# A planned hybrid transformer kernel: new charges and handoffs in the planner, and buffer fills moved from GpSimd to ScalarE

## The chip, the core and the metric

The kernel runs on one core of one Trainium2 chip. The metric is the device time of one launch in microseconds. Before the change the median of three runs is 515.56 us (514.37 to 515.59).

A core has a matrix engine (TensorE, PE in the profile, with its weight loads as PEld), a vector engine (VectorE, DVE), an activation engine (ScalarE, ACT), a general engine (GpSimd, POOL) and a queue that issues transfers (SyncE, SP). Each works through its own list of instructions in order, and waits at the head of its list for the semaphores of the others.

## What is computed

An input of 8 sequences x 256 tokens x 128 features, all in fp32, goes through eight residual layers. Cut to what matters:

```python
x = x + causal_attention(layernorm(x))      # one head of width 64, softmax
x = x + relu_ffn(layernorm(x))              # 128 -> 512 -> 128, with a layernorm at its end
x = x + linear_attention(layernorm(x))      # no softmax
x = x + relu_ffn(layernorm(x))
x = x + retention(layernorm(x))             # 16 heads, decay mask, gate
x = x + silu_ffn(layernorm(x))              # 128 -> 384 -> 128, weights from int32
x = x + softmax_attention(layernorm(x))     # 16 heads of width 8, LoRA weights
x = x + silu_ffn(layernorm(x))
```

## The kernel before, in words

**Tiles.** The 16 tiles of 128 tokens are held in four groups of four tiles, so that a group is two sequences. Each group has its buffer `x0` to `x3` (128 x 512) and goes through all eight layers as one thread, `layers(g)`. Within a layer a thread splits into more threads, such as one per sequence. PSUM is eight banks of 128 x 512; SBUF work buffers are handed out from named stores.

**The planner.** The order of the instructions is found in Python while the kernel is built. Every thread is a generator. `step(engine, us)` asks for a turn on an engine and says how long it will hold it; `either` names two engines and takes the one that is free first; `get` and `put` take buffers from a store and give them back. `Plan.run` keeps for each engine the time at which it is free, takes the earliest possible step, prefers ACT steps that need no table change and then the lower rank (group 0 first, the one-time work with rank LAST last), and lets the thread emit its instructions there. A step that follows one on another engine may start only after the first engine's entry in `HANDOFF`. What is emitted is a fixed list for each engine; the times of the plan are gone by then. So the charges do not make an instruction faster or slower: they decide which instruction stands before which on its engine, which of two engines an `either` takes, and, through the time at which a buffer comes free, which buffer and how many are taken.

**What matters for the change.**

- `constants()` (started at 8.0 us of the plan with rank LAST) fills the buffers of the later layers with ones and zeros on GpSimd: two triangles of `chunk_mul` (L379, L380), three `r_values` and three `l_values` of 128 x 576 (L388), and two halves each of two `r_spread` and two `l_spread`, 128 x 1024 a half (L392).
- `layernorm()`: statistics on DVE (L467, L468), four small GpSimd instructions for the reciprocal root (L470 to L473), and one instruction a tile on ACT (L479) or DVE (L484).
- `copied()` (L372) moves a PSUM bank to SBUF on ACT or DVE, whichever the plan has free first.
- `causal_attention()` is the first layer: weights L527 and L540, scores L562, mask L567, maxima L571, exponentials L574, transposes L581.
- `ffn_relu()` (L659, L672), `retention()` (its tiled products L795, L853, L875, L883) and `ffn_silu()` (L985, L991, L1001) follow.
- `pairs_of_scores()` is one thread for the 16-head attention of all groups. Scores of two heads are one item; an item needs two banks, and it exists twice: once for the maxima (`maxima`, L1092 on DVE) and once for the exponentials (`exponentials`, L1126 on ACT). A scoring step at L1071 takes two items, that use all four 32-row strips of PE, or one item, that uses two of them. While other groups are still at work a step with two items waits for four banks; in the last group (`todo["alone"]`) it takes two items only if more than one bank is free at that moment of the plan, and one item otherwise. A bank counts as free `LEEWAY` after its reader's step. `weighted()` (L1143) multiplies the exponentials with the values.

Each fp32 matmul stands in the profile as two records, so that a step with one item is 8 records at L1071 and a step with two items is 16.

Of the kernel before, what the change touches and what calls it, by code (L numbers as in the profile page):

```python
# [33 lines left out]
P = 128  # L34
# [28 lines left out]
HANDOFF = {PE: 0.3, ACT: 0.2, DVE: 0.2, POOL: 0.25, SP: 2.3}  # L63
TABLE_LOAD = 1.3
LEEWAY = 0.4
# [45 lines left out]
class Plan:  # L111
# [4 lines left out]
    def __init__(self):  # L116
        self.free = {e: 0.0 for e in (PE, ACT, DVE, POOL, SP)}
        self.steps = {e: [] for e in self.free}
        self.stores, self.untils, self.sleeping = [], [], []
        self.table = None  # L120
        self.current = None
        self.count = 0
        self.now = 0.0
# [25 lines left out]
    def resume(self, th, value):  # L149
# [12 lines left out]
        if kind == "step":  # L162
            for e, us, table in want[1]:
                self.steps[e].append((th.after(e), th, self.count, us, table))
        elif kind == "get":
# [18 lines left out]
    def run(self):  # L184
        self.go = []
        while True:
# [45 lines left out]
            if table not in (None, self.table):  # L232
                us += TABLE_LOAD
                self.table = table
            th.t, th.last = start + us, e
# [6 lines left out]
def step(engine, us, table=None):  # L242
    return ("step", ((engine, us, table),))


def either(*choices):
    return ("step", tuple((e, us, None) for e, us in choices))
# [19 lines left out]
def hybrid(ctx: ExitStack, tc: tile.TileContext, t: dict, out: bass.AP):  # L267
# [57 lines left out]
    nc.gpsimd.memset(minus_half, -0.5)  # L325

# [43 lines left out]
    def copied(dst, src, us):  # L370
        e = yield either((ACT, us), (DVE, us + 0.02))
# [3 lines left out]
    def constants():  # L375
# [8 lines left out]
        for store in (r_values, r_spread, l_values, l_spread):  # L384
            for _, _, tl in list(store.items):
                if tl.shape[1] == 2:
                    yield step(POOL, 0.6)
                    nc.gpsimd.memset(tl, 1.0)  # L388
                else:
                    for c in range(2):  # L390
                        yield step(POOL, 0.95)
                        nc.gpsimd.memset(tl[:, :, c, :], float(c))  # L392
        made["constants"] = True

    def causal_weights():
# [3 lines left out]
        yield step(PE, 0.5)  # L399
        nc.tensor.matmul(ps[:, :P], a_t[:, 0, :], a_t[:, 1, :], start=True, stop=True)  # L400
        nc.tensor.matmul(ps[:, P : 2 * P], a_t[:, 2, :], a_v2, start=True, stop=True)
        yield step(DVE, 0.6)
# [5 lines left out]
    def linear_weights():  # L408
# [3 lines left out]
        yield step(PE, 0.3)  # L412
        nc.tensor.matmul(ps[:, :P], b_tp[:, 1, :], b_tp[:, 0, :], start=True, stop=True)
        yield step(DVE, 0.3)
# [4 lines left out]
    def retention_weights():  # L419

        for w in (w_ret_vg, b_ret_v):
            yield step(DVE, 0.9)
# [8 lines left out]
    def silu_weights():  # L431
        ws = []
        for wi in (wi_gate, wi_up, wi_down):
            w = wi.bitcast(F32)
            yield step(DVE, 0.75)
# [5 lines left out]
    def softmax_weights():  # L441
# [3 lines left out]
        yield step(PE, 0.7)  # L445
# [4 lines left out]
        yield step(DVE, 0.8)  # L450
# [8 lines left out]
    def layernorm(src, y):  # L459
# [5 lines left out]
        for i in range(nt):  # L465
            yield step(DVE, 0.45)
            nc.vector.bn_stats(stats[:, i, :], src[:, i, :])  # L467
            nc.vector.bn_aggr(mv[:, i, :], stats[:, i, :])  # L468
        yield step(POOL, 1.05 + 0.18 * nt)
# [5 lines left out]
        def half(tiles):  # L475
            for i in tiles:
                e = yield either((ACT, 0.49), (DVE, 0.38))
# [14 lines left out]
    def transposed(y):  # L492
# [4 lines left out]
        yield step(PE, 0.02 + 0.11 * nt)  # L497
        for i in range(nt):
            nc.tensor.transpose(ps[:, i * P : (i + 1) * P], y[:, i, :], ident)  # L499
        yield from copied(yT[:, : nt * P], ps[:, : nt * P], 0.16 + 0.11 * nt)  # L500
# [14 lines left out]
    def add_row_to(g, row):  # L515
        yield step(POOL, 1.27)
        nc.gpsimd.tensor_tensor(x[g], x[g], tokens(row, NT), ALU.add)

    def add_to(g, tiles, ps):
        xs = flat(x[g][:, tiles, :])  # L520
        yield step(DVE, 0.09 + 0.135 * (tiles.stop - tiles.start))
# [10 lines left out]
    def causal_attention(g):  # L532
# [4 lines left out]
        def queries():  # L537
# [3 lines left out]
            yield from copied(q[:, :N], ps, 0.6)  # L541
            put(bank, ps)

        def value():
            ps = yield get(bank)
            yield step(PE, 0.86)
            by_tiles(ps, w[:, 1, :], yT)
            yield from copied(values[:, :N], ps, 0.6)
            put(bank, ps)

        def sequence(b):
# [14 lines left out]
            yield step(DVE, 0.48)  # L566
            nc.vector.tensor_tensor(p[:, : 3 * P], ps[:, : 3 * P], causal_add, ALU.add)  # L567
            put(bank, ps)
            yield step(DVE, 0.55)
            for i, (q0, lo, hi) in enumerate(blocks):  # L570
                nc.vector.tensor_reduce(nmax[:, i : i + 1], p[:, lo:hi], AX.X, ALU.max, negate=True)  # L571
            yield step(ACT, 1.3, "exp")
# [6 lines left out]
            yield step(PE, 0.34)  # L579
            for i in range(3):  # L580
                nc.tensor.transpose(ps[:, i * P : (i + 1) * P], p[:, i * P : (i + 1) * P], ident)  # L581
            yield from copied(pT[:, : 3 * P], ps[:, : 3 * P], 0.48)
            put(bank, ps)
            put(work, p)
            yield step(DVE, 0.17)
            nc.vector.reciprocal(sums, sums)
            ps = yield get(bank)
            yield step(PE, 0.65)
# [6 lines left out]
            yield step(DVE, 0.55)  # L595
# [15 lines left out]
    def linear_attention(g):  # L611
# [4 lines left out]
        for left in (None, b_g, made["linear"]):  # L616
            ps = yield get(bank)
            yield step(PE, 0.86 if left is None else 0.45)
# [12 lines left out]
            yield from copied(m[:, : 2 * D], ps[:, : 2 * D], 0.37)  # L631
            put(bank, ps)
        ps = yield get(bank)
        yield step(PE, 0.86)
# [9 lines left out]
    def ffn_relu(g):  # L644
# [5 lines left out]
        def biases():  # L650
            yield step(POOL, 1.27)
# [3 lines left out]
        def up(c):  # L655
# [4 lines left out]
            e = yield either((ACT, 0.69), (DVE, 0.67))  # L660
# [6 lines left out]
        def down(tiles):  # L667
            ps = yield get(bank)
            for n, i in enumerate(tiles):
                yield step(PE, 0.88)  # L670
# [5 lines left out]
            yield step(DVE, 0.35)  # L676
# [10 lines left out]
        yield step(POOL, 1.27)  # L687
        nc.gpsimd.tensor_tensor(y4, y4, tokens(gamma, NT), ALU.mult)
        yield step(DVE, 0.62)
# [3 lines left out]
    def spread_heads(qk, b, spread):  # L693

        for i in range(4):
            yield step(SP, 0.5)
# [17 lines left out]
    def retention(g):  # L714
# [4 lines left out]
        def rotated(i):  # L719
# [17 lines left out]
            e = yield either((POOL, 1.27), (DVE, 0.62))  # L737
# [3 lines left out]
        def gated(c):  # L741
# [5 lines left out]
            yield step(ACT, 0.62, "silu")  # L747
# [3 lines left out]
        def value(b):  # L751
            v = yield get(r_values)

            def part(m):
                ps = yield get(bank)
                yield step(PE, 0.45)
# [5 lines left out]
                yield step(DVE, 0.35)  # L762
# [10 lines left out]
        def scores(b, s):  # L773
# [4 lines left out]
            def masked(i, ps):  # L778
                yield step(DVE, 0.62)
# [7 lines left out]
            for i2 in range(2):  # L787
                ps = yield get(bank, 2)
                yield step(PE, 0.95)
# [14 lines left out]
        def states(b, v, state):  # L804
# [3 lines left out]
            yield step(PE, 0.24)  # L808
# [575 lines left out]
```

## Time and profile before

| | us |
|---|---|
| median of three runs | 515.56 |
| the profiled execution | 516.39 |
| its span, first to last instruction | 514.7 |
| PE busy | 465.5 (90%) |
| DVE busy | 354.2 (69%) |
| ACT busy | 238.9 (46%) |
| POOL busy | 144.4 (28%) |
| mean granted PE clock | 0.933 of full |

Busy time is the sum of an engine's instruction spans; the ends of matmuls are modelled. The granted clock is the share of its full clock that PE was given; at half of it a matmul takes about twice as long. A bracket such as `[0.17 <-POOL small L472]` at the end of a timeline line is the idle time of that engine just before the instruction, and what ended it.

### The profile page before, as it was taken

The numbers are of one execution on the slowest core, as the hardware profiler recorded it, in microseconds if no ns is written. First come the engines' busy times: TensorE is split into PE (matmuls) and PEld (weight loads), VectorE is DVE, ScalarE is ACT, GpSimd is POOL, SyncE is SP. The second block draws the span as 40 slices with busy tenths as digits, with TensorE's granted clock in tenths as the row PEclk, the third lists the DMA queues.
The fourth block names the chain that finished last, engine by engine and source line by source line (L and its number), as shares of the span: only waits on it lengthen the run. The fifth ranks groups of instructions, "written<-read, shape, count | busy, mean of one in ns | idle before, by whom it ended". The sixth has DMA issues, their size and how long they took to land.

```text
span 514.7 us, 13048 instructions
## 1 busy us (share of the span) xinstructions
PE 465.5 (90%) x5340; PEld 320.9 (62%) x5340; DVE 354.2 (69%) x985; ACT 238.9 (46%) x477; POOL 144.4 (28%) x259
## 2 busy tenths in 40 slices
PE   2779889999779998899999999999799979999996
PEld 1666767757647667547666656676476647765654
DVE  6979885889696669959648986745975643850233
ACT  3245447343335152338656285554338465135561
POOL 6805388576334161332120020320011030010011
PEclk9979989999989999969999999999979999655899
DMA  8100000003003002001000102011000003000000
GB/s 293 62 2 1 1 1 1 0 1 43 6 0 43 3 19 29 1 7 31 16 20 4 23 11 33 4 36 24 1 2 22 12 2 54 3 1 2 11 1 21
DMA packets 8043, 10.90 MB, mean 21 GB/s; under 512 B 1000, under 2 KB 6888, under 8 KB 7984
## 3 DMA queue, kind: packets, MB, share of 16 engines
q1 hardware_dynamic: 7904, 9.94, 8.6%
q8 instruction: 42, 0.69, 0.6%
q14 instruction: 17, 0.14, 0.1%
q10 hardware_dynamic: 80, 0.13, 0.1%
HBM read 4.56 MB, written 1.05 MB: 11 GB/s over the span
## 4 chain that ended last, share of the span: by engine, by line
PE 69%; DVE 22%; issue 3%; POOL 2%; ACT 1%; DMA 1%; SPq 0%; POOLq 0%; DVEq 0%; ACTq 0%
PE bank L1071 16%; PE bank L1143 6%; PE bank L659 5%; PE bank L985 5%; DVE small L1092 4%; PE bank L1001 4%; PE bank L991 4%; PE bank L672 3%; PE bank L795 3%; DVE work L484 3%; PE bank L853 3%; PE bank L499 2%; DVE small L467 2%; PE bank L527 2%; DVE small L468 2%
## 5 line engine op out<-in xcount | busy, mean ns | idle before, releaser
L1071 PE MATMUL bank<-l_spread 32*128 32x256 f32 x1024 | 104.3, 443 | 3.6 <-DVE small L1092 3.2
L1092 DVE TENSOR_REDUCE small<-bank 128x2 f32<-128x512 f32 x128 | 80.3, 682 | 27.8 <-PE bank L1071 27.6
L1126 ACT ACTIVATE probs<-bank 128x512 f32<-128x512 f32 x128 | 68.0, 599 | 48.3 <-PE bank L1071 44.7
L1071 PEld LDWEIGHTS bank<-l_spread 32*128 32x128 f32 x1024 | 66.7, 205 | 33.1 <-issue 12.9
L470 POOL TENSOR_SCALAR small<-small 128x4 f32<-128x4 f32 (+1 forms) x44 | 10.8, 246 | 265.4 <-DVE small L468 264.4
L372 ACT COPY work<-bank 128x512 f32<-128x512 f32 (+3 forms) x76 | 36.2, 481 | 85.6 <-PE bank L499 24.7
L479 ACT ACTIVATE work<-x,small 128x128 f32<-128x128 f32 x71 | 31.2, 488 | 29.1 <-POOL small L473 28.9
L472 POOL TENSOR_TENSOR small<-small,mhalf 128x4 f32<-128x4 f32 (+1 forms) x44 | 43.2, 982 | 0.0
L372 DVE COPY work<-bank 128x512 f32<-128x512 f32 (+3 forms) x36 | 19.8, 555 | 26.2 <-PE bank L1143 12.8
L467 DVE BATCH_NORM_STATS2 small<-x 128x6 f32<-128x128 f32 x128 | 34.6, 270 | 4.0 <-DMA x<-in_x 3.7
L499 PE MATMUL bank<-ident,work 128*128 128x128 f32 x128 | 25.1, 306 | 12.5 <-ACT work L479 9.3
L484 DVE TENSOR_SCALAR work<-x,small 128x128 f32<-128x128 f32 x57 | 30.4, 747 | 5.9 <-POOL small L472 5.9
L1143 PE MATMUL bank<-probs,l_values 128*32 128x256 f32 x512 | 33.6, 398 | 0.2 <-DVE work L780 0.2
L985 PE MATMUL bank<-work,c_ints 128*128 128x256 f32 (+1 forms) x72 | 30.0, 535 | 3.5 <-ACT work L372 1.6
L468 DVE BATCH_NORM_AGGREGATE small<-small 128x2 f32<-128x6 f32 x160 | 29.1, 182 | 5.6
L659 PE MATMUL bank<-work,c_relu 128*128 128x512 f32 x64 | 31.5, 617 | 0.9 <-ACT work L372 0.9
L672 PEld LDWEIGHTS bank<-c_relu,work 128*128 128x128 f32 x256 | 30.1, 192 | 2.6 <-issue 1.9
L672 PE MATMUL bank<-c_relu,work 128*128 128x128 f32 x256 | 31.4, 277 | 0.1
L993 DVE TENSOR_TENSOR work<-bank,work 128x256 f32<-128x256 f32 (+1 forms) x36 | 17.6, 507 | 18.4 <-PE bank L991 18.2
L499 PEld LDWEIGHTS bank<-ident,work 128*128 128x128 f32 x128 | 15.7, 149 | 23.2 <-ACT work L479 13.6
L1001 PEld LDWEIGHTS bank<-c_ints,work 128*128 128x128 f32 x192 | 23.9, 191 | 5.7 <-issue 3.2
L1001 PE MATMUL bank<-c_ints,work 128*128 128x128 f32 x192 | 26.7, 283 | 0.8 <-DVE work L993 0.8
(146 smaller groups left out, 807.1 us busy)
## 6 DMA issues: line engine op xcount, KB each, us to landing
r_spread<-wide SPq DMA_DIRECT2D x32, 64.0 KB
l_spread<-wide SPq DMA_DIRECT2D x32, 64.0 KB
out<-x SPq DMA_DIRECT2D x8, 128.0 KB
c_retention_qk<-in_retention_qk SPq DMA_DIRECT2D x1, 770.0 KB
x<-in_x SPq DMA_DIRECT2D x3, 256.0 KB
c_retention_vo<-in_retention_vo SPq DMA_DIRECT2D x1, 713.0 KB
c_relu<-in_relu SPq DMA_DIRECT2D x1, 706.0 KB
c_ints<-in_ints SPq DMA_DIRECT2D x1, 576.0 KB
```

The lines of the kernel that those rows point to most:

```text
L372: (nc.scalar.copy if e == ACT else nc.vector.tensor_copy)(dst, src)
L467: nc.vector.bn_stats(stats[:, i, :], src[:, i, :])
L484: nc.vector.tensor_scalar(y[:, i, :], src[:, i, :], mv[:, i, 0:1], rstd[:, i : i + 1], ALU.subtract, ALU.mult,)
L499: nc.tensor.transpose(ps[:, i * P : (i + 1) * P], y[:, i, :], ident)
L659: nc.tensor.matmul(ps, w1[:, c * P : (c + 1) * P], yT[:, :N], start=True, stop=True)
L672: nc.tensor.matmul(ps[:, n * D : (n + 1) * D], h[c][:, i * P : (i + 1) * P], w2[:, c, :], start=(c == 0), stop=(c == 3),)
L985: nc.tensor.matmul(ps[:, :n], w_gate[:, cols], yT[:, :n], start=True, stop=True)
L1001: nc.tensor.matmul(ps[:, (i - first) * D : (i - first + 1) * D], h[c][:, i * P : (i + 1) * P], w_down[:, c, :], start=(c == 0), stop=(c == 2),
L1071: nc.tensor.matmul(to[k][:, n * S : (n + 1) * S], seq.spread[rows, j, of_keys, n * P : (n + 1) * P], seq.spread[rows, j, 1 - of_keys, :], ...
L1092: nc.vector.tensor_reduce(nmax[:, h2 % 4 // 2, 2 * (h2 % 2) + k, :], ps[k].rearrange("p (m s) -> p m s", m=2), AX.X, ALU.max, negate=True,)
L1126: nc.scalar.activation(p[:, k, :], ps[k], AF.Exp)
L1143: nc.tensor.matmul(o[32 * i : 32 * (i + 1), (j % 2) * S : (j % 2 + 1) * S], seq.v[:, c, VONE * h : VONE * h + 32], seq.p[h2][0][:, k, c * ...
```

## The change

**Fills.** In `constants()` the six fills of 128 x 576 and the eight of 128 x 1024 become ScalarE copies from a 128 x 2 tile `levels`, read with a stride of zero. `levels` is written by two GpSimd memsets of 128 x 1 near the start. The triangles of `chunk_mul` stay on GpSimd.

**Handoffs and charges.** The planner's handoffs become shorter, `LEEWAY` is halved, and nearly every `step` gets another charge. A PSUM copy's charge is now worked out from its number of columns. The other large ones: the exponentials of a 128 x 512 bank 0.60 to 0.49, a layernorm tile on ACT 0.49 to 0.39 and on DVE 0.38 to 0.25, the exponentials of a causal sequence 1.3 to 0.89, the scoring step of L1071 0.80 to 0.99, a spread transfer's issue on SP 0.50 to 0.74.

**Tiling.** PE steps carry a `mode`. The planner adds 0.09 where the mode is another than that of the PE step before, and otherwise 0.1 where the step came later than 0.1 before PE was free. The rule by which a step is chosen doesn't look at the mode.

No matmul, no element-wise instruction other than the fills, no buffer and no transfer is added or removed.

```diff
-HANDOFF = {PE: 0.3, ACT: 0.2, DVE: 0.2, POOL: 0.25, SP: 2.3}
+HANDOFF = {PE: 0.2, ACT: 0.15, DVE: 0.13, POOL: 0.1, SP: 2.0}
 TABLE_LOAD = 1.3
-LEEWAY = 0.4
+NEW_MODE = 0.09
+LOAD = 0.1
+LEEWAY = 0.2
+def of_act(n):
+    return 0.05 + n / 1160
+def of_dve(n):
+    return 0.066 + n / 960
...
+            if e == PE:
+                if th.mode != self.mode:
+                    us += NEW_MODE
+                elif q[0] > self.free[e] - LOAD:
+                    us += LOAD
+                self.mode = th.mode
...
+    levels = buffer("levels", [P, 2])
+    for c in range(2):
+        nc.gpsimd.memset(levels[:, c : c + 1], float(c))
...
-    def copied(dst, src, us):
-        e = yield either((ACT, us), (DVE, us + 0.02))
+    def copied(dst, src, n):
+        e = yield either((ACT, of_act(n)), (DVE, of_dve(n)))
...
-                    yield step(POOL, 0.6)
-                    nc.gpsimd.memset(tl, 1.0)
+                    yield step(ACT, of_act(576))
+                    nc.scalar.copy(flat(tl), levels[:, 1:2].to_broadcast([P, 2 * tl.shape[2]]))
                 else:
                     for c in range(2):
-                        yield step(POOL, 0.95)
-                        nc.gpsimd.memset(tl[:, :, c, :], float(c))
+                        yield step(ACT, of_act(4 * S))
+                        nc.scalar.copy(tl[:, :, c, :], levels[:, c : c + 1].unsqueeze(1).to_broadcast([P, 4, S]))
...
-        yield step(POOL, 1.05 + 0.18 * nt)
+        yield step(POOL, 1.14 + 0.16 * nt)
...
-                e = yield either((ACT, 0.49), (DVE, 0.38))
+                e = yield either((ACT, 0.39), (DVE, 0.25))
...
-            yield step(ACT, 1.3, "exp")
+            yield step(ACT, 0.89, "exp")
...
-            yield step(SP, 0.5)
+            yield step(SP, 0.74)
...
-                yield step(PE, 0.95)
+                yield step(PE, 0.94, mode="row tiles")
...
-                yield step(PE, 0.8)
+                yield step(PE, 0.8, mode="tiles")
...
-            yield step(PE, 1.0)
+            yield step(PE, 0.93, mode="column halves")
...
-            yield step(PE, 0.8)
+            yield step(PE, 0.99, mode="row tiles")
...
-            yield step(ACT, 0.6, "exp")
+            yield step(ACT, 0.49, "exp")
...
-            yield step(PE, 0.9)
+            yield step(PE, 0.89, mode="column tiles")
```

## The prediction

> **What bounds the kernel now.** I read the busy times first, then the timeline of the first 40 us, then the last 80 us. PE is busy 465.5 of 514.7 us, so a gain has to come from the 49.2 us in which PE idles or from PE time lost to a slow clock. The profile's second part shows where they lie:
>
> ```profile
> PE   2779889999779998899999999999799979999996
> DVE  6979885889696669959648986745975643850233
> POOL 6805388576334161332120020320011030010011
> PEclk9979989999989999969999999999979999655899
> ```
>
> A digit covers 12.9 us. Early on PE is a 2 and two 7s while POOL has a 6 and an 8; near the end PE is at 9 with its clock at 6, 5, 5. The 20 us windows put PE's idle time at 14.9 us up to 40 us, 26.3 us from 60 to 420 us and 4.9 us after 500 us.
>
> The early timelines (start, duration, engine, line, operation) of POOL and DVE say why:
>
> ```profile
> 15.09 0.58 POOL L388 MEMSET r_values<- 128x576 f32 x1
> 15.61 3.63 POOL L392 MEMSET r_spread<- 128x1024 f32 x4
> 19.17 1.62 POOL L388 MEMSET l_values<- 128x576 f32 x3
> 20.73 3.64 POOL L392 MEMSET l_spread<- 128x1024 f32 x4
> ```
>
> ```profile
> 14.91 9.86 DVE L484 TENSOR_SCALAR work<-x,small 128x128 f32<-128x128 f32 x3 [1.13 <-POOL small L472]
> 24.69 0.54 DVE L567 TENSOR_TENSOR work<-bank,causal_add 128x384 f32<-128x384 f32 x1
> ```
>
> One 128x128 normalisation takes 9.537 us (the longest of L484's 57) where the median is 0.340 us. It ends as the fills end, at 24.37 us. Everything behind it on DVE, the causal masks first, waits. PE has other work up to 22.97 us and then pays:
>
> ```profile
> 24.51 0.66 PE L499 MATMUL bank<-ident,work 128*128 128x128 f32 x4 [1.53 <-DVE work L484]
> 26.14 0.33 PE L581 MATMUL bank<-ident,work 128*128 128x128 f32 x1 [0.56 <-ACT work L574]
> 26.63 0.44 PE L581 MATMUL bank<-ident,work 128*128 128x128 f32 x2 [0.17 <-ACT work L574]
> 29.61 2.08 PE L527 MATMUL bank<-a_w,work 128*128 128x128 f32 x8 [2.55 <-DVE work L372]
> ```
>
> That is 4.81 us of idle PE, and the windows then show its clock at 0.72, 0.50, 0.50 and 0.57 between 28 and 36 us; PE is busy from 30 to 36 us, which costs it 1.0 + 1.0 + 0.86 = 2.9 us.
>
> The second place is the last group's softmax attention. Windows of 2 us have the clock at 0.50 from 442 to 478 us with PE busy nearly all the time. PE's timeline there shows scoring steps one item at a time:
>
> ```profile
> 461.47 2.08 PE L1071 MATMUL bank<-l_spread 32*128 32x256 f32 x8
> ...
> 486.44 1.13 PE L1071 MATMUL bank<-l_spread 32*128 32x256 f32 x8
> 487.50 0.66 PE L1156 MATMUL bank<-ident,work 128*128 128x128 f32 x4
> 488.08 1.15 PE L1071 MATMUL bank<-l_spread 32*128 32x256 f32 x16
> ```
>
> A step of 8 records (one item) takes 1.06 us from start to start, as long as one of 16 records (two items, 1.08); at half clock it takes 2.0. From 435 to 497 us I count 240 records of L1071: one step of 16 and 28 of 8.
>
> [...]
>
> **The fills.** Removed from POOL: 6 x 0.58 + 8 x 0.957 = 11.1 us. With them goes the stall, 9.54 - 0.34 = 9.2 us of DVE. For PE it is worth at most its idle time and lost clock above, 4.8 + 2.9 = 7.7 us, since it worked through the rest of the stall. Added to ACT: between the 128x256 copy (0.369) and the 128x512 copy (0.585) a column costs 0.84 ns and the fixed part is 0.153 us, so a fill costs 0.64 or 1.02 us: 6 x 0.64 + 8 x 1.02 = 12.0 us. ACT is busy 3.1 of 12.8 us and then 5.8 of 12.9 us, so it has room up to 39 us; retention, which needs the buffers, first reads them beyond 100 us. But a fill isn't interrupted. Queued behind it can be normalised tiles (L479), PSUM copies and the exponentials L574, and PE waits for those. The cost lies between 0 and about 5 us (every fill half in the way of something: 14 x 0.43 = 6, less what isn't on the path); I take 2.2. A fill's table is one that any copy uses, so no table load. The two 128x1 memsets before the first POOL work at 5.10 us cost about 0.1 us each of idle POOL: nothing; without that idle time 0.2 us. Sum: 7.7 - 2.2 = 5.5 us, between 2 and 8.
>
> **The charges in the first 420 us.** They add no instruction. They move plan and chip closer: a layernorm tile on ACT lasts 0.49 and PE starts 0.05 later (497.23 to 497.72, then 497.77); the old plan allowed 0.49 + 0.20, the new one 0.39 + 0.15 = 0.54, as measured. A scoring step counted 0.80 where 1.08 is measured; now 0.99 + 0.09. For the at least 64 steps of that kind that is 64 x 0.28 = 18 us of PE time the old plan didn't know of, so that it expected scores early, and put their readers early: DVE sits 27.6 us and ACT 44.7 us at the head of their queues for L1071. Every engine's order changes, so do the SP issues (0.50 to 0.74 charged, 0.69 measured): a spread transfer that moves ahead of or behind another on SP shifts a sequence by about 0.7 us. PE's 26.3 idle us are the most that can be won. No row says how many are, and an order can also lose: I take a tenth, 2.5 us, with 8 us either way. If PE stays supplied, what is late next is DVE's run of maxima (four at 2.4 us in the chain of waits), which no charge shortens.
>
> **The last group.** After the maxima are over (461 us), PE runs 11 single steps and one double one up to 497 us, and is busy 19.5 and 19.6 of 20 us: it bounds. The old plan charged 0.60 + 0.60 for an item's exponentials and 0.80 for its step, so ACT seemed the slower and one pair of banks came free at a time. Now they count 0.98 and 1.08: PE seems the slower, banks pile up, and the rule takes two items. The halved LEEWAY pushes the same way. Pairing all 11 saves 3 steps at 2.0 and 2.5 at 1.06 = 8.7 us; I take a bit under half, 4.0 us, between 0 and 9. Before 461 us DVE bounds the maxima (two at 1.28 us an item against 1.06), so I expect single steps there still, and the half clock.
>
> **Sum.** The profiled execution took 516.39 us, 1.7 of it around the span: 516.39 - 5.5 - 2.5 - 4.0 = 504.4. The median of the runs lies 0.83 below that execution, so 503.6 us is forecast, with an own range of 497 to 509.
>
> **The rivals.**
>
> - Only the stall goes; the reordering is a wash and the last group still scores singly. For it: PE is at 9 tenths nearly everywhere, and the old order wasn't starved. Against: 18 us of unplanned PE time. 515.6 - 5.5 = 510 us; if the fills on ACT eat most of the gain, up to 515.
> - The half-clock stretch at the end shrinks too. For it: the clock came back at 478.6 us, when PE had just run the 32 records of L1143, so mixed work ends it. Against: nothing in the charges aims at it. Half of its 36.7 us at full clock would save 36.7 / 2 / 2 = 9 us more: 494 us.
> - Slower: PE's true price, known to the plan, holds the last group back behind the ranks before it, and more of its 32 items are scored alone under half clock. Each then costs 2.0 us in place of its 0.54 share of a double step, 1.46 more. With the 5.5 us of the start given back by 4 of them, it decides from 5 on; 8 cost 11.7 us: 515.6 - 5.5 + 11.7 = 521.8. For it: the clock falls under such steps even with PE busy. Against: shorter charges and handoffs for DVE and ACT let the last group advance, too.
>
> **How the numbers follow.** Chances: forecast 0.48, stall only 0.22, clock too 0.13, slower 0.17. The measurement can tell about 0.3% (1.5 us) from no change. Faster by over that: 0.48 + 0.13 and 0.19 of the 0.22 = 0.80; within it 0.05 (the fills take the gain back, or three or four more single steps do); slower 0.15. The range runs from 491 (the bounds of the last group and of the order both at their better side, or half of the clock case) to 517 (stall only with costly fills, and the mild part of the slower case); about 2 in 10 lie outside.
>
> **What would show it.** Right: no L484 above about 1.5 us before 40 us, fills at about 0.64 and 1.02 us on ACT, PE's clock above 0.9 from 25 to 39 us, PE idle under 11 us before 40 us; steps of 16 at L1071 in the last 60 us; idle PE from 60 to 420 us below 26 us. Wrong: PE waiting for ACT behind fills in the first 40 us, as many single steps or more at the end, or a half-clock stretch longer than 37 us.

## The result, and the profile after

The changed kernel takes 476.44 us (median of four runs, 474.57 to 480.46) against 514.97 us for the kernel before beside it (median of four, 514.37 to 515.59): a ratio of 0.926, 95% interval 0.920 to 0.932. The forecast was 503.6 us with a range of 491 to 517. The profiled execution took 476.66 us with a span of 474.9. Medians and ranges below are over all runs; a ratio with an interval leaves out runs more than 1.5% above their kernel's fastest, which is why it can differ from the quotient of the medians.

The same four rows as before from the profile's second part (a digit is now 11.9 us):

```profile
PE   3989989879979997999999999998899999899996
DVE  6699777779839894899667957774858674595223
POOL 6106867494702563133211111311002012010011
PEclk9999999989989999999999999998979999999999
```

PE starts with 3, 9, 8 where it had 2, 7, 7, POOL's 8 in the second slice is a 1, and the 6, 5, 5 of the clock near the end are nines. To add up the parts, I split the span with the granted clock: PE's work at full clock (busy time less half of the time at half clock, the little of it in which PE idled included), its idle time, and the time lost to the clock. The 20 us windows give

| PE's work at full clock, done by | before | after | after leads by |
|---|---|---|---|
| 40 us | 21.7 us | 29.8 us | 8.1 us |
| 200 us | 164.9 us | 171.7 us | 6.8 us |
| 400 us | 344.7 us | 359.9 us | 15.2 us |
| the end | 430.9 us at 514.7 | 428.8 us at 474.9 | 39.8 us of span |

So the start gives 8, the stretch from 40 to 400 us gives 7, and what comes after 400 us gives 24.6: there the old kernel needs 114.7 us for 86.2 us of work, and the new one 74.9 for 68.9. Of the 24.6 us, 19.3 are clock: after 400 us the old kernel's PE ran 38.6 us at half clock, the new one's none. Another 3.2 us are idle time (9.2 against 6.0).

**The start.** ACT's timeline of the changed kernel has the fills, with exponentials (L595) behind the last:

```profile
12.11 1.80 ACT L409 COPY r_values<-levels 128x576 f32<-128x576 f32 x3
13.81 1.04 ACT L413 COPY r_spread<-levels 128x1024 f32<-128x1024 f32 x1
...
18.32 2.94 ACT L413 COPY r_spread<-levels 128x1024 f32<-128x1024 f32 x3
21.15 1.24 ACT L409 COPY l_values<-levels 128x576 f32<-128x576 f32 x2
...
23.25 0.69 ACT L409 COPY l_values<-levels 128x576 f32<-128x576 f32 x1
23.82 3.89 ACT L413 COPY l_spread<-levels 128x1024 f32<-128x1024 f32 x4
27.60 0.41 ACT L595 ACTIVATE work<-work,small 128x128 f32<-128x128 f32 x1
```

DVE's timeline has four normalisations in 1.11 us in the place of the stall, and the causal mask comes at 19.72 instead of 24.69 us:

```profile
16.73 1.11 DVE L505 TENSOR_SCALAR work<-x,small 128x128 f32<-128x128 f32 x4
19.06 0.69 DVE L393 COPY work<-bank 128x512 f32<-128x512 f32 x1 [1.22 <-PE bank L561]
19.72 0.56 DVE L588 TENSOR_TENSOR work<-bank,causal_add 128x384 f32<-128x384 f32 x1
```

PE's timeline goes on without the gaps of 0.5 to 2.6 us that it had here:

```profile
21.48 1.04 PE L520 MATMUL bank<-ident,work 128*128 128x128 f32 x8
22.45 0.48 PE L434 MATMUL bank<-c_linear 32*128 32x128 f32 x2
22.93 1.16 PE L548 MATMUL bank<-a_w,work 128*128 128x128 f32 x8
```

**The end.** PE's timeline of the last group, first of the changed kernel (L1092 is the scoring step), then of the kernel before:

```profile
409.97 1.13 PE L1092 MATMUL bank<-l_spread 32*128 32x256 f32 x8
411.03 0.70 PE L1006 MATMUL bank<-work,c_ints 128*128 128x256 f32 x2
411.66 1.13 PE L1092 MATMUL bank<-l_spread 32*128 32x256 f32 x8
412.72 0.71 PE L548 MATMUL bank<-c_softmax,work 128*128 128x128 f32 x4
413.36 1.13 PE L1092 MATMUL bank<-l_spread 32*128 32x256 f32 x8
```

```profile
436.88 4.23 PE L1071 MATMUL bank<-l_spread 32*128 32x256 f32 x32
441.04 0.28 PE L1105 MATMUL bank<-ident,small 128*16 128x128 f32 x1
441.25 5.59 PE L1071 MATMUL bank<-l_spread 32*128 32x256 f32 x32
```

Both still score one item at a time for the most part. But the new order mostly has a product of another layer between two scoring steps, while the old one scored four items in a row from 436.88 us on, then four more; its clock fell at 441.9 us. Windows over each kernel's last group hold 256 records of scoring both times, with 42.5 us busy at a mean clock of 0.71 before and 29.3 us at 1.00 after.

### The profile page after: what moved, and what is told of

The parts are those of the page before. It is cut to its first block, busy times and chain, and to the rows that moved or that the text cites. A ratio compares the mean times of both kernels' runs of the same rounds, so it can differ in the third digit from the quotient of the medians.

```text
span 474.9 us, 13095 instructions
## 1 busy us (share of the span) xinstructions
PE 437.3 (92%) x5340; PEld 303.3 (64%) x5340; DVE 341.0 (72%) x975; ACT 254.7 (54%) x505; POOL 133.1 (28%) x245
## 4 chain that ended last, share of the span: by engine, by line
PE 68%; DVE 13%; POOL 4%; issue 4%; ACT 3%; ACTq 0%; DVEq 0%; POOLq 0%
PE bank L1092 16%; PE bank L1164 6%; PE bank L1006 4%; PE bank L693 4%; PE bank L680 4%; PE bank L1022 4%; PE bank L1012 4%; PE bank L874 3%; DVE small L1113 3%; PE bank L749 2%; PE bank L816 2%; PE bank L904 2%; PE bank L959 2%; PE bank L520 2%; PE bank L1177 2%
## 5 line engine op out<-in xcount | busy, mean ns | idle before, releaser
L1113 DVE TENSOR_REDUCE small<-bank 128x2 f32<-128x512 f32 x128 | 80.8, 681 | 29.5 <-PE bank L1092 29.3
L1092 PE MATMUL bank<-l_spread 32*128 32x256 f32 x1024 | 89.3, 409 | 0.5 <-ACT probs L1147 0.3
L1092 PEld LDWEIGHTS bank<-l_spread 32*128 32x128 f32 x1024 | 55.7, 188 | 24.9 <-issue 14.7
L500 ACT ACTIVATE work<-x,small 128x128 f32<-128x128 f32 x79 | 34.0, 485 | 28.9 <-POOL small L494 28.7
L1164 PE MATMUL bank<-probs,l_values 128*32 128x256 f32 x512 | 32.0, 388 | 1.7 <-ACT work L1008 1.7
L683 ACT ACTIVATE work<-bank,c_relu 128x512 f32<-128x512 f32 x30 | 20.6, 686 | 21.0 <-PE bank L680 21.0
L393 DVE COPY work<-bank 128x512 f32<-128x512 f32 (+3 forms) x33 | 18.5, 564 | 17.2 <-PE bank L520 4.9
L520 PE MATMUL bank<-ident,work 128*128 128x128 f32 x128 | 23.3, 294 | 6.9 <-ACT work L500 5.8
L1006 PE MATMUL bank<-work,c_ints 128*128 128x256 f32 (+1 forms) x72 | 26.2, 479 | 2.4 <-ACT work L393 2.4
L1012 PE MATMUL bank<-work,c_ints 128*128 128x256 f32 (+1 forms) x72 | 25.2, 460 | 0.1
```

What stands on the lines that cost most here:

```text
L393: (nc.scalar.copy if e == ACT else nc.vector.tensor_copy)(dst, src)
L1006: nc.tensor.matmul(ps[:, :n], w_gate[:, cols], yT[:, :n], start=True, stop=True)
L1012: nc.tensor.matmul(ps[:, :n], w_up[:, cols], yT[:, :n], start=True, stop=True)
L1092: nc.tensor.matmul(to[k][:, n * S : (n + 1) * S], seq.spread[rows, j, of_keys, n * P : (n + 1) * P], seq.spread[rows, j, 1 - of_keys, :], ...
L1113: nc.vector.tensor_reduce(nmax[:, h2 % 4 // 2, 2 * (h2 % 2) + k, :], ps[k].rearrange("p (m s) -> p m s", m=2), AX.X, ALU.max, negate=True,)
L1164: nc.tensor.matmul(o[32 * i : 32 * (i + 1), (j % 2) * S : (j % 2 + 1) * S], seq.v[:, c, VONE * h : VONE * h + 32], seq.p[h2][0][:, k, c * ...
```

## The experiments

The kernel before was run 55 more times beside these kernels, on the chips of their runs. Its times spread from 491.4 to 518.7 us (median 509.7), but span times granted clock only from 476.5 to 485.2 us; the rest is clock loss, 7 to 37 us. So times alone compare badly, and this table gives the two parts into which the span falls. (PE's idle time at half clock counts half in the first.)

| kernel | runs | us, median (range) | span x clock, mean (range) | clock loss, mean (range) | ratio to before, 95% |
|---|---|---|---|---|---|
| before | 55 | 509.7 (491.4 to 518.7) | 481.3 (476.5 to 485.2) | 26.1 (6.9 to 36.7) | |
| after, first chip | 4 | 476.4 (474.6 to 480.5) | 466.3 (465.5 to 467.1) | 8.9 (5.7 to 12.4) | 0.926 (0.920 to 0.932) |
| after again | 4 | 477.0 (475.4 to 480.6) | 467.0 (464.6 to 468.8) | 8.8 (5.2 to 12.5) | |
| fills alone | 4 | 490.1 (486.1 to 492.2) | 473.7 (472.6 to 475.5) | 14.0 (8.7 to 17.6) | 0.968 (0.960 to 0.975) |
| charges alone | 4 | 483.4 (478.8 to 495.2) | 461.8 (459.4 to 465.9) | 21.7 (17.7 to 27.6) | 0.952 (0.944 to 0.960) |
| handoffs alone | 4 | 490.6 (489.5 to 491.9) | 469.9 (468.1 to 472.0) | 19.1 (17.1 to 22.1) | |
| score price alone | 20 | 514.0 (494.8 to 518.4) | 486.3 (483.9 to 489.4) | 21.7 (3.9 to 31.5) | 0.984 (0.977 to 0.991) |
| after, old handoffs | 4 | 485.4 (484.1 to 487.1) | 473.0 (471.2 to 474.9) | 10.6 (10.1 to 11.1) | 0.966 (0.957 to 0.975) |
| after, old score price | 4 | 479.4 (478.5 to 486.6) | 462.1 (460.7 to 463.5) | 17.2 (14.3 to 24.2) | 0.953 (0.946 to 0.959) |
| before, doubles at end | 5 | 491.9 (491.2 to 500.1) | 475.9 (474.7 to 477.9) | 15.8 (13.7 to 20.4) | 0.972 (0.966 to 0.979) |
| before, added products | 4 | 500.4 (500.0 to 502.6) | 489.7 (488.3 to 490.6) | 9.5 (8.5 to 12.5) | |
| after, maxima first | 4 | 482.9 (480.3 to 490.2) | 466.6 (466.0 to 467.3) | 15.7 (12.0 to 22.5) | |
| before, PE 0.31 | 4 | 507.2 (503.2 to 508.1) | 483.8 (480.6 to 487.3) | 21.0 (18.6 to 25.8) | |
| before, DVE 0.21 | 4 | 502.6 (499.9 to 513.3) | 482.8 (479.4 to 485.0) | 20.1 (13.9 to 32.2) | |
| after, PE 0.21 | 4 | 477.6 (475.8 to 482.1) | 463.3 (461.4 to 465.2) | 13.0 (11.9 to 15.4) | |
| after, DVE 0.14 | 4 | 484.3 (479.8 to 488.0) | 471.4 (468.1 to 472.8) | 10.7 (5.3 to 15.5) | |
| after, doubles at end | 6 | 477.0 (474.5 to 479.8) | 463.4 (461.2 to 464.5) | 11.7 (8.5 to 15.2) | 0.957 (0.947 to 0.966) |
| after, old score price, doubles | 6 | 482.6 (478.4 to 483.4) | 463.9 (462.9 to 466.0) | 16.0 (13.8 to 18.3) | 0.966 (0.957 to 0.975) |

### What lowers PE's clock

My theory after the result was that the clock follows how much of the array works. The first kernel runs steps of that kind alone:

```diff
+    dense(24)                      # 24 products of 128x128 by 128x512
+    for k in range(24):
+        scores(k, (0, 1) if k % 2 == 0 else (2, 3))      # single steps
+    dense(24)
+    for k in range(24):
+        scores(k, range(4))                              # double steps
+    dense(24)
+    for k in range(20):
+        scores(k, (0, 1) if k % 2 == 0 else (2, 3))
+        nc.tensor.matmul(banks[k % 8][:, :S], w1[:, :P], flat[k % 4][:, :S], start=True, stop=True)
```

> The kernel leaves out the whole computation: it loads x, copies it out unchanged, and between runs only matmuls on it, in stages of some 20 to 26 us with dense 128x512 products before and after each: single scoring steps (two of four 32-row strips), double steps (all four strips), single steps each followed by one full 128x256 product, and 32-column products. Theory A (the PE clock falls when the array is little occupied, even with PE busy): the clock is at 0.5 through the stage of single steps after its first few us, a step goes from 1.06 to about 2.0 us, and the clock stays at 1.0 in the other three stages. Theory B (only idle time of PE lowers the clock): no stage falls below 1.0, all single steps take 1.06 us.

Theory A failed: the clock was at 1.00 throughout. But the single steps that alternate between the strips overlapped and took 10.75 us for 24, 0.45 each; only those with a full product on either side took 1.06 us here, as Theory B had expected of all. Nothing held them back as VectorE does in the kernel. So the next one paced them:

```diff
+    for k in range(32):
+        scores(k // 2, pair(k))
+        read(k // 2, pair(k))          # two maxima on VectorE
...
+        if k >= 16:
+            nc.tensor.matmul(banks[7][:, :S], w1[:, :P], flat[k % 4][:, :S], start=True, stop=True)
```

> Leaves out the whole computation: loads x, copies it out unchanged, and runs only matmuls and maxima on it, in stages between stretches of dense products: (1) 36 single scoring steps all on the same two strips; (2) 80 single steps that alternate between the two pairs of strips, back to back; (3) 32 single steps each read by two maxima on VectorE, so that banks coming free pace PE at about 1.24 us a step; (4) 16 double steps paced likewise at 2.5 us; (5) 16 single steps on three pairs of banks paced by maxima, then 16 with one full 128x256 product after each. Theory A (PE's clock follows how much of the array works, and the profile's busy time hides that a paced PE mostly waits): the clock is 0.5 in most of stages 1 and 3 and in the first half of 5, a single step there takes 2.0 us, and the clock stays at 1.0 in 2, in the second half of 5. Theory B (what lowered it in the kernel was idle time elsewhere): it stays at 1.0 in all stages.

Four windows over its stages show, in this order, single steps on the same strips unpaced, single steps paced by maxima, double steps paced, and single steps each with a full product behind. Behind the window and its length stand the busy times of PE, PEld, DVE and POOL, then the granted clock.

```profile
33.20:64.50 31.30, 31.30 (x290) 27.53 (x289) 0.00 (x0) 0.00 (x0) 1.00 0.01 2
...
150.00:177.00 27.00, 27.00 (x183) 26.91 (x179) 27.00 (x46) 0.00 (x0) 0.50 0.00 1
210.00:236.00 26.00, 26.00 (x176) 21.76 (x175) 26.00 (x44) 0.00 (x0) 0.57 0.00 1
281.00:329.00 48.00, 48.00 (x152) 25.69 (x152) 20.07 (x32) 0.00 (x0) 0.50 0.00 1
```

Unpaced, half of the strips are enough for the full clock: occupancy isn't it. Paced by VectorE, the clock falls within 6 to 8 us, for double steps too, although PE is shown busy all the time. The 80 unpaced alternating steps took 34.9 us, 0.44 each; paced they took 1.15. So in the paced stage, as an estimate from these times, PE had work for less than half of the time at full clock, and its busy time hides that. The last stage is the surprise. The same mix of a single step and a 128x256 product stood in the first clock kernel, entered at full clock (VectorE does nothing there, so its column is missing):

```profile
106.20:140.00 33.80, 33.80 (x202) 19.82 (x202) 0.00 (x0) 1.00 0.00 0
```

There it kept full clock for all of its 33.8 us, at 1.69 us a step. Entered at half clock, after paced steps, it stayed at half for 48 us, at 3.16 us a step. The two stages differ in one more thing: in the second each step is still read by two maxima. They don't pace PE, for VectorE sits idle for 1.87 us before each pair of them until PE is ready:

```profile
287.02 1.29 DVE L374 TENSOR_REDUCE small<-bank 128x2 f32<-128x512 f32 x2 [1.87 <-PE bank L369]
```

Dense 128x512 products brought the clock back 2.3 to 5.6 us after they began.

In the whole kernel before, first without most of the single steps at the end, then with work added between them:

```diff
-            if len(chosen) == 2 and not todo["alone"]:
+            if len(chosen) == 2:
```

> The kernel before with one edit: in the last group a step with two items waits for four banks as it does earlier, so that steps of 16 records replace most single ones. Theory A (occupancy): the half-clock stretch of 37 us is gone or under 10 us, and with it some 16 us; about 495 us, 488 to 503. Theory B (the stretch comes from the order of the last group as such, or from idle time): the clock still falls there, and the time stays above 508 us.

It took 491.9 us, the time that A expected, though occupancy had failed as its reason. In the profiled run, the slowest of the five, the half clock near the end lasted 10.3 us from 440.7 us on in place of 37.5, and came while VectorE paced the double steps.

```diff
+            if todo["alone"] and any(not of_keys for of_keys, _, _ in chosen):
+                nc.tensor.matmul(ps[0][0][:, :S], w1[:, :P], w1[:, :S], start=True, stop=True)
```

> The kernel before in its own order, with work added: in the last group each scoring step with an item of maxima is preceded by one 128x256 product into the bank that the step then overwrites, charged at nothing, 15 in all. Theory A (a stretch of maxima paced by VectorE drops PE's clock, and the half clock then lasts): the half-clock stretch from 442 us is gone, some 15 us of clock loss with it, against 15 x 0.45 = 7 us of added time where VectorE paces PE; 0.975 to 0.99 of before, faster for more work. Theory B (the drop comes from something else in the order): the stretch stays, and the time is 5 to 15 us above before.

The stretch is gone: after 428 us only one dip of 3.4 us is left before the one at the very end, and the loss is 8.5 or 12.5 us in each run against 6.9 to 31.0 beside it. Span times clock goes up by 8.4 us, the price of the products. In time that is 500.0 to 502.6 against 491.4 to 509.3, so the added work is free or better in the middle, and a loss against the luckiest run. That luckiest run has a clock loss of 6.9 us in all, where the stretch alone costs 18: the old order doesn't fall into it every time. Then the reverse in the changed kernel:

```diff
-            if todo["alone"] and under_way[0] > under_way[1]:
-                kinds.reverse()
+            if todo["alone"] and firsts:
+                kinds = [(firsts, 0)]
```

> The kernel after with one edit: in the last group all items of maxima that are ready go before any item of exponentials, in place of taking turns. Theory A (as above): a stretch of maxima alone comes about as in the kernel before, the half clock is back for over 10 us after 395 us, and the time goes up by 8 to 20 us over after, 0.945 to 0.97 of before. Theory B (the order of the last group isn't what keeps the clock): within 4 us of after.

Its PE timeline, from the slowest of its four runs, has a row of six items scored with nothing between them, and the steps behind are at half clock:

```profile
432.12 7.32 PE L1092 MATMUL bank<-l_spread 32*128 32x256 f32 x48
439.36 0.63 PE L1126 MATMUL bank<-ident,small 128*16 128x128 f32 x2
439.93 2.07 PE L1092 MATMUL bank<-l_spread 32*128 32x256 f32 x8
441.93 1.65 PE L1022 MATMUL bank<-c_ints,work 128*128 128x128 f32 x6
443.51 2.08 PE L1092 MATMUL bank<-l_spread 32*128 32x256 f32 x8
```

The half clock lasted 13.7 us from 437.0 us on. The cost, 6 us in the median with span times clock unchanged, is a little under what A expected, but the mechanism is the one of the kernel before.

### Which part of the change brings what

Fills on ScalarE in the kernel before, and the fills put back on GpSimd in the kernel after:

```diff
-                    yield step(POOL, 0.6)
-                    nc.gpsimd.memset(tl, 1.0)
+                    yield step(ACT, 0.55)
+                    nc.scalar.copy(flat(tl), levels[:, 1:2].to_broadcast([P, 2 * tl.shape[2]]))
```

> The kernel before with the fills on ScalarE and nothing else of the change. By 40 us PE should have done about 8 us more work at full clock than before (29.8 against 21.7). Theory A (the start is worth 8 us and is carried to the end, the rest of the gain comes from the charges): 507 us. Theory B (the start is given back later, since the last group's half-clock stretch and waits take it up): 513 to 516 us. Theory C (the order of the end is changed by chance too): the half-clock stretch at the end is shorter by over 10 us and the time under 500 us.

> The kernel after with the fills put back on GpSimd, all charges and handoffs new. Theory A (parts add): 476 + 8 = 484 us, with the long L484 of about 9 us back before 40 us and no half-clock stretch over 10 us after 380 us. Theory B (the gain of the end hangs on the exact order, which any change of the start upsets): the half-clock stretch is back and the time is above 495 us.

The fills alone took 490.1 us, and C of the first expectation is what happened. PE had done 28.0 us of work by 40 us, 6.3 more than before. Span times clock fell by 7.6 us against all runs of before, and by 5.4 against those on the same chip (479.1); 11 or 12 us more came off the clock loss, since its profile has no half clock from 244 us to 486 us. The page of that kernel:

```profile
PE   3888998869989999899899999998878999999996
PEclk9999999959989999899599999999999999999999
```

The charges alone took 483.4 us, as A expected, again with no half clock from 320 us to 493 us, but with three stretches of some 10.2 us earlier. With the fills back on GpSimd one normalisation took 10.58 us again, and the causal mask came at 24.32 us:

```profile
13.50 10.90 DVE L505 TENSOR_SCALAR work<-x,small 128x128 f32<-128x128 f32 x3 [1.20 <-POOL small L493]
24.32 0.54 DVE L588 TENSOR_TENSOR work<-bank,causal_add 128x384 f32<-128x384 f32 x1
```

Then the charges by parts. The scoring step alone at its measured price, the old handoffs in the new kernel, the old price in the new kernel, and the new handoffs alone:

```diff
-            yield step(PE, 0.8)
+            yield step(PE, 1.08)
```

> The kernel before with one number changed: the scoring step of L1071 is charged 1.08 us, as measured, in place of 0.80. Theory A (this price is what the plan lacked): most of the gain of the charges is there, 0.96 of the time before or less, and double steps stand in the last group. Theory B (handoffs and the other durations carry it): within 1.5% of before, 0.985 to 1.015. Theory C (any other order of the last group escapes the half-clock stretch): about 0.965, by the clock alone, span times clock unchanged at about 479 us.

```diff
-HANDOFF = {PE: 0.2, ACT: 0.15, DVE: 0.13, POOL: 0.1, SP: 2.0}
+HANDOFF = {PE: 0.3, ACT: 0.2, DVE: 0.2, POOL: 0.25, SP: 2.3}
-LEEWAY = 0.2
+LEEWAY = 0.4
```

> The kernel after with HANDOFF and LEEWAY as before. Theory A (the durations and the price of scoring carry the gain): within 1.5% of after, 0.925 to 0.945 of before. Theory B (the handoffs carry it): most of the charges' gain is gone, 0.96 or more of before. Theory C (any order away from the old one): span times clock goes up by some us, the clock loss stays under 20 us, about 0.945.

```diff
-NEW_MODE = 0.09
-LOAD = 0.1
+NEW_MODE = 0.0
+LOAD = 0.0
...
-            yield step(PE, 0.99, mode="row tiles")
+            yield step(PE, 0.8, mode="row tiles")
```

> The kernel after with the scoring step charged 0.80 again and with no charge for a change of tiling or a late load; all else new. Theory A (this price is what the plan lacked): 0.96 or more of before, with the half-clock stretch back in the last group. Theory B (handoffs and durations carry it): within 1.5% of after, 0.92 to 0.945.

> The kernel before with only HANDOFF and LEEWAY as after; all charges and the fills old. With the run that has the old handoffs in the kernel after (0.966) it completes the square. Theory A (handoffs and durations belong together: charge plus handoff is what a step costs until the next engine starts): small, 0.98 to 1.0 of before. Theory B (the handoffs carry most of the charges' gain): 0.955 to 0.97. Theory C (chance: any new order moves the time by a few per cent either way): outside both.

The price of scoring is not what the plan lacked: alone it made span times clock 5.0 us longer, and the median of its 20 runs, 514.0 us, is not below the 511.9 of before beside it. Without it (and the tiling charges) the new kernel kept its gain, 462.1 against 466.6 us, at 8 us more clock loss. The handoffs seem to count: alone they take 11.4 us off (0.97 of the time before, between A and B), and taking them out of the new kernel puts 6.4 us back (0.966 of before, as B expected). But the next section shows that an order by itself can move 5 to 8 us, so only the 11.4 is clear of that. The other new durations took nearly nothing off on top of the fills (473.0 against 473.7), and 8 us on top of the new handoffs (461.8 against 469.9). Parts of an order don't add.

> The kernel after, unchanged, on the chip of the runs beside it, so that they can be compared with it. 0.92 to 0.94 of before, and span times clock at about 466 us as in its first four runs; if the two parts add as factors, 0.9677 x 0.9525 = 0.922.

That run set the second row of after in the table, on a chip where before stood at 505.0 us.

### Is it the charges or the luck of an order?

Each of these changes one charge by 0.01:

```diff
-HANDOFF = {PE: 0.3, ACT: 0.2, DVE: 0.2, POOL: 0.25, SP: 2.3}
+HANDOFF = {PE: 0.31, ACT: 0.2, DVE: 0.2, POOL: 0.25, SP: 2.3}
```

> The kernel before with the handoff of PE charged 0.31 in place of 0.30: as good or bad a plan, but another order. Theory A (charges that are right make a better order): span times clock stays with the kernel before, 476 to 486 us. Theory B (the old order was an unlucky one, and any change of it helps): 475 us or less.

> The kernel before with the handoff of DVE charged 0.21 in place of 0.20. As for the run with 0.31 for PE: A, span times clock 476 to 486 us; B, 475 us or less.

> The kernel after with the handoff of PE charged 0.21 in place of 0.20. Theory A: span times clock stays with the kernel after, 461 to 471 us, time 0.92 to 0.955 of before. Theory B (the new order is a lucky one): above 471 us.

> The kernel after with the handoff of DVE charged 0.14 in place of 0.13. As for the run with 0.21 for PE: A, span times clock 461 to 471 us; B, above 471 us.

Three orders with the old charges and fills have span times clock at 481.3, 483.8 and 482.8 us, three with the new ones at 466.6, 463.3 and 471.4, the last just beyond what A allowed, so that B holds for it by the letter. The mean difference is 15.5 us, and within a kind an order moves it by up to 8. The clock loss is 26, 21 and 20 against 9, 13 and 11 us. So the change as a whole carries the difference, and the particular order a few us of it. These runs don't part the charges from the fills, which took off 5.4 to 7.6 us alone. The stretch at the end varies with the order, too: in the profiles of the two neighbours of before it lasted 13.6 us, behind ten items scored in a row from 433.96 us on, and 41.0 us. But in the two neighbours of after, and in the five other orders that keep most of the new charges (charges alone, old handoffs, old score price, and the two with doubles of the next section), no half clock after 400 us lasted longer than 10.2 us. What in the charges brings this about isn't shown.

### Doubles at the end of the new kernel

> The kernel after with the edit of the doubles at the end: in the last group a step with two items waits for four banks. Theory A (single steps leave PE open to the half clock and cost a step each): clock loss under 10 us in every run and 0 to 5 us faster than after. Theory B (waiting for four banks starves VectorE and ScalarE at the end): slower than after by 2 to 8 us.

> The kernel after with the scoring step at 0.80 and no charge for tiling changes and late loads, and with the doubles at the end. The same without the doubles had span times clock at 462 us and 14 us of clock loss. Theory A: the doubles keep the clock, loss under 10 us, time 470 to 475 us, faster than after. Theory B: slower than after.

Neither beats the kernel after: the first takes 477.0 us, with 3 us less span times clock and 3 more clock loss, and the second, with the old price, 482.6 us. No version here was clearly faster than the change.

## Why the prediction was wrong

**The start was right.** Its mechanism, the fills on GpSimd that held one L484 for 9.5 us, is gone: no normalisation takes longer than 1.31 us, and with the fills put back one takes 10.58. That they caused it I took from their common end, the last memset's at 24.37 us and the normalisation's at 24.45. The fills take 0.67 and 1.04 to 1.06 us on ACT, 12.4 us in all (12.0 forecast), with no table load before any of them, as before any of the 114 ACT copies of the kernel before; PE's idle time up to 40 us is 10.2 us (under 11), and its clock is 1.00 up to 40 us. That the dip of the clock belonged to the stall was an estimate; the runs bear it out, with 0.83 from 20 to 40 us before and with the fills put back, and 1.00 with the fills alone. I forecast 5.5 us; the fills alone gave 6.3 by 40 us, and 8.1 with the new charges. So the term for fills in the way, 2.2 us, was a little too large (7.7 less 6.3 leaves 1.4): 0.5 us on PE's weight loads behind a fill is all that the waits show.

**The charges in the first 420 us were mis-sized.** I took 2.5 us; from 40 to 400 us the lead grew by 7.1, within the 8 either way that I gave. Only 3.6 us of that are idle time, which the term was about (25.0 against 21.4 us); 3.4 are dips of the clock, which vary from run to run. The reason I gave, the 18 us of scoring that the plan didn't know of, is refuted by both runs that change that price. The shorter handoffs seem to do more.

**The last group is the step that failed.** What came after 400 us gave 24.6 us. I forecast 4.0 us by pairing items after the maxima, and wrote that before them "I expect single steps there still, and the half clock". The single steps are there, and the half clock is not. I had written down that it falls although PE is busy, and that mixed work seemed to end it, and still gave its disappearance 0.13 and only half of its size. So 19.3 us of lost clock stood in my sum at nothing. The runs put in its place: the clock falls in a row of scoring steps that VectorE paces (in the paced kernel within 6 to 8 us), and then stays down through mixed work that would have kept it up (0.50 for 48 us, against 1.00 for 33.8). The new order, with a product between most steps, had no half clock there. Shown for this are the paced kernel, the added products, and the maxima put first. Of the pairing, five steps of 16 records stand by themselves in the new timeline (419.89 to 448.38 us), two of them after the maxima, against one from 435 us on before; at 1.06 us for each step saved this is an estimate of 1 to 4 us. Forced on all items in the new kernel it brought nothing more in time. The planner knows nothing of the clock, and why orders with the new charges avoid such rows isn't shown.

**The rivals.** "The clock too" was the one that happened, with all of the stretch and not half. (The profile has the clock back at 479.4 us and not 478.6, so the stretch was 37.5 us and not 36.7; on the 494 us of that rival this is 0.2 us.) "Only the stall goes" had the right price for the start, 5.4 us of span times clock on one chip, but the fills alone gained 16 us and not 5.5, because the order of the end that came with them escaped the stretch. Not every new order does: half clock near the end still lasted 23.9 us with the score price alone, 17.1 with the handoffs alone, and 41.0 with DVE's handoff at 0.21. The slower one has no trace.

What stays open: what PE's clock follows (busy time as the profile shows it isn't it: 27.0 of 27.0 us busy had 0.50), how often the old order falls into the stretch, and which waits the shorter handoffs removed, step by step.

## What to carry to other kernels

Charges in a planner are worth trying as a set: here the shorter handoffs alone gave a better order, while the measured price of one step alone gave none. Read the granted clock beside the busy time: an engine at 100% busy at half clock may merely be paced by another one, as PE was by VectorE (27.0 of 27.0 us busy at 0.50), and an order that puts other products between paced steps can keep the clock up: 15 added products cost 8.4 us, and the mean clock loss was 9.5 us against 21.2 beside them. And judge one order against another by neighbours of both, since a change of 0.01 in one charge moves the time by some us.

## What the runs showed of the hardware

PE's clock had two lasting states under the same PE work: single scoring steps with a 128x256 product each kept 1.00 for 33.8 us when entered at full clock, and 0.50 for 48 us when entered at half; in the second each step was read by two maxima, too. The dips that end within the span lasted 3.41 us (two), 6.83 (two), 10.24 and 37.55 in the profile of before, and 3.41 (three) and 6.83 in that of after, so each was 3.41 us or a multiple of it. A PE that is shown busy throughout fell to half (27.0 of 27.0 us busy at 0.50, paced by maxima) and failed to come back (48.0 of 48.0 us busy at 0.50, with the products between).

In the kernel before a VectorE normalisation lasted 9.54 us in place of 0.34 while twelve GpSimd memsets ran in a row, from 15.09 to 24.37 us, and ended 0.08 us after the last of them. With the fills on ScalarE none lasted longer than 1.31 us, and with the fills back on GpSimd one took 10.58. How the memsets hold it up isn't shown.

A single step right behind another on the same strips took 0.87 us (36 in 31.35 us), a double step behind another 0.875 (24 in 21.0 us), and the same between products of the full array 1.06 and 1.08. The product behind the step is longer, too: a 128x256 product took 0.63 us between two steps, where half of a 128x512 product in a dense row is 0.43 (24 in 20.87 us, an estimate). From these times I estimate about 0.2 us for going from 32-row to 128-row products, and as much for going back, 0.4 in all; what takes this time isn't shown.
